# A graph network of two GINE and two GIN layers: edges counted in single tiles of 128, with up to 18 columns, and the units shared between the layers by columns

## The chip, the cores and the metric

The kernel runs on one core of a Trainium2 chip. The metric is the device time of one launch in microseconds (us), and lower is better. The core has five engines with an instruction queue each: TensorE (PE in the profile, with its weight loads as PEld), VectorE (DVE), ScalarE (ACT), GpSimd (POOL) and SyncE (SP). They wait for each other through semaphores. SP, ScalarE and GpSimd also issue transfers (DMA).

## The reference

There are N = 6250 nodes with D = 128 features, and E = 100,000 edges, sorted by their destination `dst`. Destinations are drawn as N times the square of a uniform number, so the first tiles of edges fall on few nodes and the last on more. With a layer norm and a ReLU before each half, it computes

```
h = max(layernorm(x), 0)
twice (GINE):  msg = relu(h[src] + edge_attr)              # one row of 128 per edge
               agg = segment_sum(msg, dst)
               h   = relu(relu(relu(batchnorm((h + agg) W1 + b1)) W2 + b2))
x = x + h
h = max(layernorm(x), 0)
twice (GIN):   agg = segment_sum(h[src], dst)               # no edge features
               h   = relu((1 + eps) h + agg) @ wA.T ... @ wB.T
x = x + h
```

A GINE message needs the row of its edge, so every edge's source row is gathered. A GIN message is just the source row: the sum over the edges is a product of node features with a matrix that says how many edges run from each node to each node. That matrix of counts depends on the edge list alone.

## The kernel before

*GINE layers.* Edges are taken in 98 groups of 1024 (128 partitions by G = 8 tiles). For every group, in this order: `load_rows` (SP) brings the edge features; `gather` (L638, GpSimd) issues eight indirect transfers of 128 rows into a `g` tile, of which there are eight; `places` (L647, VectorE) makes a one-hot matrix that says to which column (destination) each edge goes; `Counter.count` runs for the units that fall to this group; then `sums` adds the edge rows (L654, VectorE), applies the ReLU (L655, ScalarE) and multiplies with the one-hot on TensorE (L659, eight products in fp32, 16 passes). The sums are added into `acc`, which holds all nodes as columns, one group later (BEHIND = 1) at L690. Each engine keeps the order in which the program issues its instructions. A new gather into a `g` tile waits for the sums that read it eight groups earlier.

*Counting.* It runs beside the two GINE layers, for the first 70 groups' edges (560 tiles of 128), and prepares the GIN layers. A unit is a stretch of UE edges whose destinations span at most `plan.unit(u)` columns (at most WOVER). For each of its UT tiles, VectorE makes `lo_j` (L739: which of 128 places within a block of nodes the source has) and `at_j` (L742: which block of nodes and which column, 49 blocks by the unit's width). TensorE multiplies them (L754) into banks of 512 columns, of which there are three, so a unit takes one to three banks. The product is a matrix of counts, and VectorE adds it into the `win` tile at L730, at a column that it reads from a register. This addition is put off: `flush` for a unit is issued after the next unit's `lo_j` and `at_j` have been issued.

```
            self.at.ready(max(u - 1, 0))
            self.flush()
            ...
            for b in range(0, NB, per):
                n = min(per, NB - b)
                pa = bank_a()
                for j in range(UT):
                    nc.tensor.matmul(pa[:, : n * w], los[j], ats[j][:, b * w : (b + n) * w],
                                     start=j == 0, stop=j == UT - 1)
                self.late.append((u, b, n, w, pa))
```

A `win` tile covers a window of 256 destinations; there are 14 windows, two tiles, and ScalarE zeroes a tile (L716) before its next window, while SP stores the finished one. These clears and stores are chores, of which every unit issues two. Columns and registers come from `Places.ready` (L673): VectorE's queue loads eight values of a row (`urow` for units, `brow` for groups, `hrow` for windows) into registers, each with a check of its bounds.

*How the units are shared out.* Layer 0 counts the units before `half`, layer 1 the rest. Within a layer, `while u < last_u and (u - first_u) * (NG - 6) < (s + 1) * (last_u - first_u)` spreads them evenly over the first 92 groups.

*GIN layers.* TensorE multiplies the stored counts with the node features (L1047). The groups from the 70th on are still gathered.

*Preparation.* Before the first group, layer norm, index tables and the rows of registers are made (L427 to L566); `in_rows` (L455) turns columns into a row on one partition by products with the identity.

Of the kernel before, what the change touches and what calls it, by code (L numbers as in the profile page):

```python
# [9 lines left out]
F32 = mybir.dt.float32  # L10
# [4 lines left out]
ALU = mybir.AluOpType  # L15
AX = mybir.AxisListType

P = 128
# [13 lines left out]

KG = 70

UE = 256
UT = UE // P
UG = P * G // UE

WC = 256
WOVER = 30  # L40

QB = 7

# [1 line left out]
class Plan:  # L45
# [4 lines left out]
    def __init__(self, n_nodes: int, n_edges: int):  # L50
# [3 lines left out]
        while u < UG * KG:  # L54
            n = 1
            while u + n < UG * KG and self.reach(u * UE, (u + n + 1) * UE) <= WC:
                n += 1
# [18 lines left out]
    def unit(self, u: int) -> int:  # L76
        return min(WOVER, int(2 * np.ceil(self.reach(u * UE, (u + 1) * UE) / 2)))

# [5 lines left out]
def runs(widths):  # L84

    first = 0
    for i in range(1, len(widths) + 1):
        if i == len(widths) or widths[i] != widths[first]:
            yield first, i - first, widths[first]
            first = i  # L90
# [3 lines left out]
def gnn_kernel(ctx: ExitStack, tc: tile.TileContext, t: dict, out: bass.AP):  # L94
# [21 lines left out]
    nc = tc.nc  # L116
    x, src, dst, edge_attr = t["x"], t["src"], t["dst"], t["edge_attr_128"]
    N, E = x.shape[0], src.shape[0]
# [8 lines left out]
    NG = NGF + 1  # L127
# [8 lines left out]
    NU, NUA = KG * UG, NG * UG  # L136
# [3 lines left out]
    plan = Plan(N, E)  # L140
    windows = plan.windows
# [26 lines left out]
    code = big.tile([P, NT], F32)  # L168
    brow = const.tile([1, NG], I32)

    hrow = const.tile([1, len(windows)], I32)
# [11 lines left out]
    def chunks():  # L183

        for c in range(NCH):
            b0 = c * CB
            n0 = b0 * P
            yield c, b0, n0, min(CB * P, N - n0)
# [63 lines left out]
    def reached(end, places, edges):  # L252
        return next((at for at in places if plan.below(at * edges) >= end), None)

    gine_ends = {e: reached(e, range(1, NG), GE) for e in chunk_ends}
    counted_ends = {e: reached(e, [windows[c][0] for c in range(2, len(windows), 2)] + [NU], UE)
                    for e in chunk_ends}
    gathered_from = min(n0 for _, _, n0, _ in chunks() if n0 >= plan.above(NU * UE))

# [31 lines left out]
    def bank_e():  # L291
        return ps_e.tile([P, 512], F32, name="pe")
# [72 lines left out]
    class Steps:  # L365
# [19 lines left out]
        def end(self):  # L385
            while self.under_way:
                self.step()
# [4 lines left out]
    row = const.tile([P, 1], F32)  # L392
    nc.gpsimd.iota(row, pattern=[[0, 1]], base=-MID, channel_multiplier=1,
                   allow_small_or_imprecise_dtypes=True)
    for b in range(0, CODES, P):
        n = min(P, CODES + CODES % 2 - b)
# [30 lines left out]
    with tc.tile_pool(name="prep2", bufs=1) as pre2:  # L427
# [8 lines left out]
        lo, hi = ends[:, 3 : 3 + UG], ends[:, 3 + UG :]  # L436
# [14 lines left out]
        def in_rows(cols, name):  # L451

            p_r = bank_e()
            for i, col in enumerate(cols):
                nc.tensor.matmul(p_r[:1, i * NG : (i + 1) * NG], col, ident[:NG, :NG],  # L455
                                 start=True, stop=True)
            r = pre2.tile([1, len(cols), NG], F32, name=name)
            nc.vector.tensor_copy(r.rearrange("o c g -> o (c g)"), p_r[:1, : len(cols) * NG])
            return r

        of_group = in_rows([ends[:, i : i + 1] for i in range(3)] + [extra], "of_group")
        lo_r = in_rows([lo[:, i : i + 1] for i in range(UG)], "lo_r")
        hi_r = in_rows([hi[:, i : i + 1] for i in range(UG)], "hi_r")
        lo_u = pre2.tile([1, NUA], F32)
        nc.vector.tensor_copy(lo_u.rearrange("o (g h) -> o g h", h=UG), lo_r.rearrange("o h g -> o g h"))
        hi_u = pre2.tile([1, NUA], F32)
        nc.vector.tensor_copy(hi_u.rearrange("o (g h) -> o g h", h=UG), hi_r.rearrange("o h g -> o g h"))
        base_r, top_r = of_group[:, 0, :], of_group[:, 1, :]
        nc.vector.tensor_copy(brow, base_r)
        nc.vector.tensor_scalar_add(wrow, of_group[:, 3, :], 1.0)  # L470


# [19 lines left out]

        first_u = pre2.tile([1, NU], F32)
        for c, (a, n) in enumerate(windows):
            nc.vector.tensor_copy(hrow[:, c : c + 1], lo_u[:, a : a + 1])
            nc.vector.tensor_copy(first_u[:, a : a + n], lo_u[:, a : a + 1].to_broadcast([1, n]))
        nc.vector.scalar_tensor_tensor(diff_r[:, :NU], hi_u[:, :NU], -float(WC), first_u, op0=ALU.add,
                                       op1=ALU.subtract)
        worst(2, NU)

        n = NU - (2048 // UE - 2)
# [4 lines left out]
                                       op0=ALU.add, op1=ALU.subtract)  # L506
# [6 lines left out]
        for i, (u, end) in enumerate(early):  # L513
            nc.vector.tensor_scalar(diff_r[:, i : i + 1], lo_u[:, u : u + 1], -1.0, float(end - 1),
                                    op0=ALU.mult, op1=ALU.add)
# [4 lines left out]
        for s in range(NCH - 1 - BEHIND):  # L520
            u = UG * (s + 1) - 1
# [10 lines left out]
        def spread(r, n):  # L532

            p_b = bank_e()
            nc.tensor.matmul(p_b[:, :n], ones, r, start=True, stop=True)
            return p_b[:, :n]
# [6 lines left out]
        def by_tile(f, name):  # L543

            v = pre2.tile([P, KG, G], F32, name=name)
            for j in range(G):
                nc.vector.tensor_copy(v[:, :, j], transposed(f, j * P, 1, KG))
            return v

        s_t = by_tile(sg, "s_t").rearrange("p g j -> p (g j)")  # L550
        d_t = by_tile(dg, "d_t")
# [3 lines left out]
        block = pre2.tile([P, NT], F32)  # L555
        nc.vector.tensor_copy(block, block_i)
        nc.vector.scalar_tensor_tensor(slo, block, -float(P), s_t, op0=ALU.mult, op1=ALU.add)
        nc.vector.tensor_tensor(
            code.rearrange("p (u j) -> p u j", j=UT), d_t.rearrange("p g (h j) -> p (g h) j", j=UT),
            spread(lo_u[:, :NU], NU)[:, :, None].to_broadcast([P, NU, UT]), ALU.subtract)  # L560
        for a, n, w in runs([plan.unit(u) for u in range(NU)]):
            r = slice(a * UT, (a + n) * UT)
            nc.vector.scalar_tensor_tensor(code[:, r], block[:, r], float(w), code[:, r],
                                           op0=ALU.mult, op1=ALU.add)
# [9 lines left out]
    for name in vec_names:  # L574
        v = t[name]
        n = v.shape[0] if len(v.shape) == 2 else 1
# [24 lines left out]
    for name in ("eps1", "eps2"):  # L601
        e = t["L1_gnn_" + name]
# [60 lines left out]
    class Places:  # L663
# [5 lines left out]
        def ready(self, s):  # L669

            if s not in self.got:
                e = min(s + 8, self.row.shape[-1])
                _, got = nc.values_load_multi_w_load_instructions(  # L673
                    self.row[0:1, s:e], engines=[mybir.EngineType.DVE], min_val=0, max_val=self.most)
                self.got = dict(zip(range(s, e), got))

        def at(self, s, w):
# [19 lines left out]
    class Counter:  # L697
# [11 lines left out]
        def clear(self, c):  # L709

            if c < len(windows):
                win = self.wins[c] = self.pool.tile([P, NB, WC + WOVER], F16, name="win", bufs=2)
                flat = win.rearrange("p b w -> p (b w)").bitcast(F32)
# [231 lines left out]
    own_terms(tables[0], 1.0)  # L945
    rows, own_later = {}, []

    half = min((a for a, _ in windows), key=lambda a: abs(2 * a - NU))
    for l in range(2):

        first_stages, end = batch_norm(l)
        steps, rest = Steps(first_stages), list(chunks())
        cs = Columns(brow)
        u, first_u, last_u = (0, 0, half) if l == 0 else (half, half, NU)
        for s in range(NG):
            n = P if s < NGF else RP
            for r in range(l * NG + s, min(l * NG + s + AHEAD + 1, 2 * NG)):
                if r not in rows:
                    rows[r] = load_rows(gine, r % NG, P if r % NG < NGF else RP, AHEAD + 2)
            g = gather(edge, tables[l], n, srcs[:, s * G : (s + 1) * G], 8)  # L960
            onehot = places(edge, tables[l], dloc[:, s, :], plan.group(s))
            while u < last_u and (u - first_u) * (NG - 6) < (s + 1) * (last_u - first_u):
                counter.count(u)
                u += 1
                if u == NU:
                    counter.end()
            counter.some_chores()
            if own_later:

                got = None  # L970
                for stage in own_stages:
                    got = stage(*own_later[0], got)
                own_later.pop(0)
            cs.ready(max(s - BEHIND, 0))
            cs.later(s, sums(g, n, onehot, rows.pop(l * NG + s)), BEHIND)
            rows[l * NG + s] = None
            steps.step()
            ready = gine_ends[rest[0][2] + rest[0][3]]
            if ready is not None and ready <= s + 1 - BEHIND:
                steps.begin(rest.pop(0))  # L980
            if l == 0 and s == AHEAD:
                unplanned = nc.values_load(total[0:1, 0:1], min_val=0, max_val=1)
        if l:
            ahead[:] = chunks()
            load_ahead(x)
        while cs.late:
            cs.add(*cs.late.pop(0))
        for chunk in rest:
            steps.begin(chunk)
            steps.step()  # L990
        steps.end()
        if l == 0:
            own_stages = gine_nodes(0, *end())[:3]
            staged(*gine_rows(tables[1], own_stages[0]))
            own_later = list(chunks())
# [13 lines left out]
    queue, tiles = [(l, c, q) for l in range(2) for c, q in order], {}  # L1009
# [82 lines left out]
    for l in range(2):  # L1092
# [37 lines left out]
        for s in range(KG, NG):  # L1130
            n = P if s < NGF else RP
            g = gather(gin, tables[2 + l], n, srcs[:, s * G : (s + 1) * G], 4)
# [107 lines left out]
```

## Time and profile before

| what | us |
|---|---|
| median of 3 runs | 3341.68 (3339.88 to 3350.18) |
| the profiled execution's own time | 3338.77 |
| its span, first to last instruction | 3336.8 |
| first gather of GINE layer 0, last gather | 41.4, 1195.8 |
| first gather of GINE layer 1, last gather | 1267.3, 2434.7 |
| last addition into `acc` of layer 1 | 2471.6 |
| TensorE, VectorE, ScalarE, GpSimd busy | 1820.7, 1382.5, 455.4, 2035.1 |

The mean TensorE clock that was granted is 0.764 of full speed. The first 148 us or so are preparation, 41 to 2472 us the two GINE layers with the counting beside them (their start overlaps with the preparation), and the rest the GIN layers.

How to read the profile: a row of the costliest groups has the line, the engine, the operation, output <- inputs, the shape and the number of instructions; after the bar, busy time in all, mean ns of one, and idle time of the engine just before them with what ended most of it. "Issue" means that nothing the profile shows was waited for, and "remote" that the waking event belongs to no engine the profile can name. In the waits a row says which instruction waited for which, how long in total, how often, and the longest. In the timeline a line has the start, the duration (several instructions in one line are joined), the engine and line, and in brackets the idle time before and its releaser. Ends of matmuls are modelled.

### The profile page before, as it was taken

What the parts mean: (1) busy time and instruction counts of PE and PEld (TensorE: products, weight loads), DVE (VectorE), ACT (ScalarE), POOL (GpSimd) and SP (SyncE); (2) the same over time, 40 slices, a digit from 0 to 9 for tenths busy, and PEclk for the clock granted to TensorE, in tenths of its full rate; (3) what the DMA queues carried; (4) which work ended last, traced back from release to release, by engine and by line L of the source; (5) the groups of instructions that cost most, each with busy time, mean ns of one, the idle gap of its engine ahead of it and who ended that gap; (6) DMA issues with size and microseconds to landing.
All of it is one profiled execution on the core that took longest, in us unless ns stands there. A gap on an engine that the chain in (4) does not pass through costs nothing. (4 is left out here: it accounts for less than half of the span.)

```text
span 3336.8 us, 28904 instructions
## 1 busy us (share of the span) xinstructions
PE 1820.7 (55%) x8459; PEld 1143.3 (34%) x8460; DVE 1382.5 (41%) x3051; ACT 455.4 (14%) x579; POOL 2035.1 (61%) x2118
## 2 busy tenths in 40 slices
PE   1333424444444453365555564455558688857997
PEld 0233423332323242243333343332334344423443
DVE  5322424334445542255555666677753111211112
ACT  1200101010101121111101111111122101110000
POOL 6467666666667736666766666666614566545662
PEclk9999999995666665555555656666778888878998
DMA  3332323234224224242442443343447455545664
GB/s 117 121 95 89 100 79 95 88 92 127 90 88 134 90 69 139 69 128 89 135 128 82 128 134 119 118 133 119 125 136 236 137 170 185 184 136 183 224 219 128
DMA packets 259236, 421.94 MB, mean 126 GB/s; under 512 B 40864, under 2 KB 187088, under 8 KB 259068
## 3 DMA queue, kind: packets, MB, share of 16 engines
q1 hardware_dynamic: 173532, 184.05, 17.8%
q0 software_dynamic: 71424, 146.03, 14.7%
q10 hardware_dynamic: 14112, 89.92, 7.6%
q8 instruction: 69, 1.13, 0.1%
q14 instruction: 99, 0.81, 0.1%
HBM read 352.48 MB, written 67.36 MB: 126 GB/s over the span
## 5 line engine op out<-in xcount | busy, mean ns | idle before, releaser
L638 POOL DMA_INDIRECT g<-table,srcs x2016 | 1982.6, 983 | 1095.2 <-issue 913.2
L659 PE MATMUL pe<-onehot,g 128*128 128x16 f32 (+25 forms) x4480 | 751.8, 338 | 603.8 <-ACT g L655 339.7
L659 PEld LDWEIGHTS pe<-onehot,g 128*128 128x128 f32 x3136 | 621.7, 300 | 657.7 <-ACT g L655 406.3
L754 PE MATMUL pa<-at_j,lo_j 128*128 128x450 f16 (+22 forms) x1172 | 423.1, 488 | 644.1 <-DVE win L730 246.8
L1047 PE MATMUL pa<-piece,xp 128*128 128x512 f16 x2058 | 496.8, 394 | 75.7 <-issue 73.3
L730 DVE TENSOR_TENSOR win<-win,pa 128x450 f32 (+17 forms) x586 | 316.3, 574 | 494.9 <-remote 363.7
L754 PEld LDWEIGHTS <-lo_j 128*128 128x128 f16 x1172 | 155.0, 138 | 858.0 <-issue 521.8
L655 ACT ACTIVATE g<-g 128x1024 f32<-128x1024 f32 x196 | 207.0, 1056 | 1599.2 <-DVE g L654 773.9
L742 DVE TENSOR_SCALAR at_j<-numbers,code 128x1470 f16<-128x1470 f16 (+13 forms) x560 | 362.9, 648 | 0.0
L690 DVE TENSOR_TENSOR acc<-acc,pe 128x112 f32 (+18 forms) x252 | 61.2, 243 | 692.4 <-remote 288.6
L1047 PEld LDWEIGHTS <-xp 128*128 128x128 bf16 x2058 | 204.0, 100 | 360.7 <-issue 155.2
L654 DVE TENSOR_TENSOR g<-g,rows 128x1024 f32<-128x1024 f32 x196 | 238.8, 1218 | 81.1 <-issue 46.1
L647 DVE TENSOR_TENSOR onehot<-numbers,dloc 128x896 bf16<-128x896 f32 (+23 forms) x252 | 224.4, 890 | 9.0 <-issue 9.0
L739 DVE TENSOR_SCALAR lo_j<-numbers,slo 128x128 f16<-128x128 f16 x560 | 153.5, 274 | 2.1 <-issue 2.1
L659 PEld LDWEIGHTS <-g 128*128 128x128 bf16 (+1 forms) x1344 | 87.9, 103 | 80.5 <-issue 57.3
L716 ACT COPY win<-zero 128x1001 f32<-128x1001 f32 x98 | 92.9, 1018 | 74.0 <-remote 74.0
L690 DVE TENSOR_TENSOR acc<-acc,pa 128x256 f32 x28 | 11.8, 422 | 180.2 <-PE pa L1047 109.0
L799 DVE BATCH_NORM_STATS2 bst<-pn 128x6 f32<-128x512 f32 (+1 forms) x26 | 17.3, 666 | 164.7 <-remote 89.4
L918 ACT ACTIVATE y<-pn,vcols 128x512 f32<-128x512 f32 (+1 forms) x26 | 17.1, 658 | 473.3 <-PE pn L331 421.7
L319 POOL TENSOR_SCALAR h<-xs,rs 128x128 f32<-128x128 f32 x49 | 21.3, 447 | 90.7 <-DVE rs L312 84.5
L826 DVE TENSOR_TENSOR xs<-xs,pn 128x512 f32<-128x512 f32 (+1 forms) x26 | 17.0, 654 | 71.0 <-PE pn L347 44.0
L1101 DVE TENSOR_TENSOR h<-pn,xp 128x512 f32<-128x512 f32 (+1 forms) x13 | 8.6, 658 | 90.8 <-ACT xp L1100 68.5
(162 smaller groups left out, 640.8 us busy)
## 6 DMA issues: line engine op xcount, KB each, us to landing
rows<-in_edge_attr SPq DMA_DIRECT2D x194, 512.0 KB
piece<-counts ACTq DMA_DIRECT2D x98, 896.0 KB
counts<-win SPq DMA_DIRECT2D x98, 448.0 KB
g<-table,srcs POOLq DMA_INDIRECT x2016
table<-xp SPq DMA_DIRECT2D x24, 384.0 KB
x_first<-in_x SPq DMA_DIRECT2D x8, 384.0 KB
table<-x_first SPq DMA_DIRECT2D x8, 384.0 KB
xs<-table SPq DMA_DIRECT2D x12, 256.0 KB
```

The lines of the kernel that those rows point to most:

```text
L638: nc.gpsimd.indirect_dma_start(out=g[:n, j, :], out_offset=None, in_=table, in_offset=bass.IndirectOffsetOnAxis(ap=idx[:n, j : j + 1], axi ...
L647: nc.vector.tensor_tensor(onehot, cols[:, None, :w].to_broadcast([P, G, w]), dl[:, :, None].to_broadcast([P, G, w]), ALU.is_equal)
L654: nc.vector.tensor_add(g[:n], g[:n], rows[:n])
L655: nc.scalar.activation(g[:n], g[:n], AF.Relu)
L659: nc.tensor.matmul(pe, g[:n, j, f : f + D], onehot[:n, j, :], start=(j, f) == terms[0], stop=(j, f) == terms[-1])
L690: nc.vector.tensor_add(a, a, sums)
L716: self.chores.append(lambda v=flat[:, q * n : (q + 1) * n], n=n: nc.scalar.copy(v, self.zero.to_broadcast([P, n])))
L730: nc.vector.tensor_add(v, v, pa[:, : n * w].rearrange("p (b w) -> p b w", w=w))
L739: nc.vector.tensor_scalar(lo_j, cols16[:, MID : MID + P], slo[:, col : col + 1], None, op0=ALU.is_equal)
L742: nc.vector.tensor_scalar(at_j[:, :width], cols16[:, :width], code[:, col : col + 1], None, op0=ALU.is_equal)
L754: nc.tensor.matmul(pa[:, : n * w], los[j], ats[j][:, b * w : (b + n) * w], start=j == 0, stop=j == UT - 1)
L1047: nc.tensor.matmul(pa, xp[:, q * QB + b, i * D : (i + 1) * D], v[:, :, b, :], start=q + b + i == 0, stop=q == NQ - 1 and b == QB - 1 and i ...
```

## The change

A unit becomes one tile of 128 edges (UE = 128, UT = 1), so there are 560 units where there were 280, and its width is at most 18 columns where it was at most 30. Widths are now 4, 6, ... 18 along the edges, where they were 4 to 30. A unit takes one bank up to width 10 and two above. `at_j` and `lo_j` have two buffers each where they had four (2 * UT). The `win` tile is 274 columns wide for each block where it was 286.

Units are shared out by cost, where a unit's cost is its width plus 3. Layer 0 now takes 343 of the 560 tiles and layer 1 217; before, it was 132 units (264 tiles) and 148 units (296 tiles). Within a layer the units are spread over the groups by the same cost.

The rows of registers are clamped to their bounds on the chip where they are made (`brow`, `hrow`; `urow` was already), and the loads of registers skip their check.

In the preparation, the rows of first and last destinations of the units are made in two pieces each, since a bank holds five rows of 98, and the code of each tile is made in pieces of 512 units.

```diff
-UE = 256
+UE = 128
 UT = UE // P
 UG = P * G // UE
 
 WC = 256
-WOVER = 30
+WOVER = 18
...
-        lo_r = in_rows([lo[:, i : i + 1] for i in range(UG)], "lo_r")
-        hi_r = in_rows([hi[:, i : i + 1] for i in range(UG)], "hi_r")
-        lo_u = pre2.tile([1, NUA], F32)
-        nc.vector.tensor_copy(lo_u.rearrange("o (g h) -> o g h", h=UG), lo_r.rearrange("o h g -> o g h"))
-        hi_u = pre2.tile([1, NUA], F32)
-        nc.vector.tensor_copy(hi_u.rearrange("o (g h) -> o g h", h=UG), hi_r.rearrange("o h g -> o g h"))
+
+        def of_units(v, name):
+
+            row = pre2.tile([1, NUA], F32, name=name)
+            h = 512 // NG
+            for i in range(0, UG, h):
+                k = min(h, UG - i)
+                part = in_rows([v[:, j : j + 1] for j in range(i, i + k)], f"{name}_{i}")
+                nc.vector.tensor_copy(row.rearrange("o (g h) -> o g h", h=UG)[:, :, i : i + k],
+                                      part.rearrange("o h g -> o g h"))
+            return row
+
+        lo_u, hi_u = of_units(lo, "lo_u"), of_units(hi, "hi_u")
         base_r, top_r = of_group[:, 0, :], of_group[:, 1, :]
-        nc.vector.tensor_copy(brow, base_r)
+        nc.vector.tensor_scalar(brow, base_r, float(N), 0.0, op0=ALU.min, op1=ALU.max)
...
-            nc.vector.tensor_copy(hrow[:, c : c + 1], lo_u[:, a : a + 1])
+            nc.vector.tensor_scalar(hrow[:, c : c + 1], lo_u[:, a : a + 1], float(N), 0.0,
+                                    op0=ALU.min, op1=ALU.max)
...
-        nc.vector.tensor_tensor(
-            code.rearrange("p (u j) -> p u j", j=UT), d_t.rearrange("p g (h j) -> p (g h) j", j=UT),
-            spread(lo_u[:, :NU], NU)[:, :, None].to_broadcast([P, NU, UT]), ALU.subtract)
+        for a in range(0, NU, 512):
+            n = min(512, NU - a)
+            tiles = slice(a * UT, (a + n) * UT)
+            nc.vector.tensor_tensor(
+                code[:, tiles].rearrange("p (u j) -> p u j", j=UT),
+                d_t.rearrange("p g j -> p (g j)")[:, tiles].rearrange("p (u j) -> p u j", j=UT),
+                spread(lo_u[:, a : a + n], n)[:, :, None].to_broadcast([P, n, UT]), ALU.subtract)
...
                 _, got = nc.values_load_multi_w_load_instructions(
-                    self.row[0:1, s:e], engines=[mybir.EngineType.DVE], min_val=0, max_val=self.most)
+                    self.row[0:1, s:e], engines=[mybir.EngineType.DVE], min_val=0, max_val=self.most,
+                    skip_runtime_bounds_check_because="the row is clamped to these bounds on chip")
...
-    half = min((a for a, _ in windows), key=lambda a: abs(2 * a - NU))
+    cost = np.cumsum([0] + [plan.unit(u) + 3 for u in range(NU)])
+    half = min((a for a, _ in windows), key=lambda a: abs(2 * cost[a] - cost[NU]))
     for l in range(2):
...
-            while u < last_u and (u - first_u) * (NG - 6) < (s + 1) * (last_u - first_u):
+            while u < last_u and (cost[u] - cost[first_u]) * (NG - 6) < (s + 1) * (
+                    cost[last_u] - cost[first_u]):
                 counter.count(u)
                 u += 1
```

## The prediction

> **What bounds the kernel now.** I read the page's costliest groups, then the busy time by stretch, then the waits, and last the timeline.
>
> ```profile
> L638 POOL DMA_INDIRECT g<-table,srcs x2016 | 1982.6, 983 | 1095.2 <-issue 913.2
> L754 PE MATMUL pa<-at_j,lo_j 128*128 128x450 f16 (+22 forms) x1172 | 423.1, 488 | 644.1 <-DVE win L730 246.8
> L730 DVE TENSOR_TENSOR win<-win,pa 128x450 f32 (+17 forms) x586 | 316.3, 574 | 494.9 <-remote 363.7
> L690 DVE TENSOR_TENSOR acc<-acc,pe 128x112 f32 (+18 forms) x252 | 61.2, 243 | 692.4 <-remote 288.6
> ```
>
> GpSimd issues eight gathers per group of 1024 edges. A gather takes 0.94 us and the next starts 0.30 us later, so a group costs at least 10.0 us there. Beside it run the row addition, the sums and the counting. The busy time by stretch, for two stretches of each GINE layer (PE, PEld, DVE, ACT, POOL):
>
> ```profile
> 225.00:791.00 566.00, 231.70 (x942) 186.76 (x943) 201.23 (x507) 52.73 (x52) 387.98 (x392) 0.97 0.32 97
> 791.00:1118.00 327.00, 139.41 (x618) 101.30 (x618) 157.25 (x329) 45.44 (x47) 228.02 (x225) 0.63 0.32 100
> 1426.00:1588.00 162.00, 92.17 (x336) 59.01 (x336) 88.70 (x188) 28.79 (x33) 110.52 (x112) 0.54 0.36 110
> 1588.00:2347.00 759.00, 416.03 (x1606) 266.75 (x1606) 482.86 (x888) 121.88 (x126) 503.33 (x505) 0.60 0.39 121
> ```
>
> Divide each length by its groups (gathers over eight): 11.55, 11.63, 11.57 and 12.02 us a group, while VectorE is busy 4.1, 5.6, 6.3 and 7.65 us of it. No engine is full, and more VectorE work hardly shows until the last stretch. What fills the rest is in the waits:
>
> ```profile
> DVE win L730 <- remote: 363.7, 48, 23.1
> DVE acc L690 <- remote: 330.0, 24, 43.1
> ```
>
> "Remote" names no engine. The timeline shows what it is:
>
> ```profile
> 368.27 3.48 PE L659 MATMUL pe<-onehot,g 128*128 128x40 f32 x16
> ...
> 388.11 0.20 DVE L690 TENSOR_TENSOR acc<-acc,pe 128x40 f32 x1 [21.99 <-remote]
> ...
> 388.82 0.94 POOL L638 DMA_INDIRECT g<-table,srcs  x1 [4.40 <-issue]
> ```
>
> TensorE had done these sums by 371.8, but VectorE goes on only at 388.11, after GpSimd ran out of free g buffers and stood 4.40 us. The recorded increments of TensorE's semaphore come 3.5 to 6.3 us apart from 370 to 387, then 0.04 us apart. So the work falls into clear stretches, in which hand-overs are prompt, and blocked ones, in which TensorE's completions are posted late until GpSimd stalls. GpSimd stalls over 1 us 33 times in layer 0 (4.39 us on average over its normal step) and 46 times in layer 1 (3.39). The other delays of gathers come to 32 to 34 us a layer, so a group costs about 10.3 us of gathering plus its share of a stall: over a layer's 98 groups 10.3 + 33x4.39/98 = 11.8 and 10.3 + 46x3.39/98 = 11.9. The number of stalls sets the pace.
>
> In a clear stretch a group with two units looks like this:
>
> ```profile
> 389.98 1.20 DVE L654 TENSOR_TENSOR g<-g,rows 128x1024 f32<-128x1024 f32 x1
> ...
> 391.26 1.06 ACT L655 ACTIVATE g<-g 128x1024 f32<-128x1024 f32 x1 [24.00 <-DMA g<-table,srcs]
> ...
> 392.37 3.63 PE L659 MATMUL pe<-onehot,g 128*128 128x40 f32 x16 [2.27 <-ACT g L655]
> ...
> 395.81 1.18 PE L754 MATMUL pa<-at_j,lo_j 128*128 128x294 f16 x4
> 396.54 0.46 DVE L730 TENSOR_TENSOR win<-win,pa 128x294 f32 x1 [2.60 <-PE pa L754]
> 397.01 1.23 DVE L654 TENSOR_TENSOR g<-g,rows 128x1024 f32<-128x1024 f32 x1
> ```
>
> The next row addition is queued on VectorE behind the window addition of the group's first unit, whose matmul is queued on TensorE behind the last group's sums: 7.03 us from addition to addition, in series. A group with one unit flushes a unit whose matmul precedes those sums; its row addition does not wait, and two groups are in flight. The shortest intervals between row additions, stretch by stretch of 14 groups, are in layer 0 2.4 to 4.5 us with one unit and 7.0 to 8.0 with two (middle 3.5 and 7.5), in layer 1 4.1 to 6.0 and 8.3 to 10.2 (5.1 and 9.2). All intervals: in layer 0 17.8 mean with two units (39 groups), 6.9 with one (52); in layer 1 16.7 (56) and 7.6 (36).
>
> **What the Trainium skill says.** "TensorE: Matmul & The Clock Gate", The cost: per-tile semaphore tail: increments on completion serialize at 26.3 ns each. The trace agrees in clear stretches (0.04 us) and is a hundred times off in blocked ones. "GPSIMD Engine Reference", Specifications: GpSimd shares its SBUF interfaces with VectorE. The trace fits: a gather beside a row addition takes 1.94 us (390.06). "VectorE: DVE Perf Modes", Why PSUM operands drop a tier: a PSUM operand halves the fast rate, and fp32 runs at one. The rows agree: at_j (fp16) has a slope of 0.52 ns per column, the window addition 0.87.
>
> **The change part by part.** Counted from the plan, which fixes widths and order.
>
> *Less column work.* at_j has 295,960 columns where it had 474,712. By the rows (0.207 + 0.00052 us per column for at_j, 0.234 + 0.00087 for an addition) counting costs VectorE 291 -> 440 us in layer 0 and 569 -> 436 in layer 1: level in sum, moved to layer 0. VectorE's whole work per group becomes about 7.4, 7.0, 6.7, 7.2 us along layer 0 and 6.9 in layer 1 (late layer 1 had 7.65 to 9.6). On VectorE's load alone, late layer 1 falls from 12.02 to 11.6: 0.42 us x 63 groups = -27 us. I take -10, since this stretch also has longer chains than the others; kept: -30 to 0. Matmuls go from 372 to 397 and from 800 to 434.
>
> *More hand-overs.* 280 units become 560. Units per group: layer 0 from 1.43 to 5.6, 4.5, 3.4, 2.8 (14, 14, 35, 29 groups); layer 1 from 1.6 to 2.36. So every group now has two or more, and every row addition stands behind a window addition that waits for the last group's sums. A further narrow unit adds lo_j 0.19, at_j 0.28, addition 0.38 (start to start near 392) = 0.85 us; with two banks about 1.4 to 1.5. Clear chain in layer 0: 7.0 + 3.6x0.85 = 10.1; 7.0 + 2.5x0.85 = 9.1; 7.4 + 1.4x1.4 = 9.4; 7.6 + 0.8x1.5 = 8.8; weighted 9.3, where it was 0.57x3.5 + 0.43x7.5 = 5.2. Layer 1: about 8.4 (two banks to add in place of three) + 0.36x1.9 = 9.1, where it was 0.4x5.1 + 0.6x9.2 = 7.6.
>
> *What that does to stalls.* Two estimates. (1) Groups per stall are 98/33 = 2.97 at a chain of 5.2 and 98/46 = 2.13 at 7.6. If a clear stretch lasts U and p groups get through a blocked one: U/5.2 + p = 2.97, U/7.6 + p = 2.13, so U = 13.8, p = 0.31. At 9.3: 1.79 groups, 55 stalls, +22x4.39 = +97 us in layer 0. At 9.1: 1.83, 54 stalls, +8x3.39 = +27 in layer 1. (2) By waits: 48 remote waits at window additions in 95 two-unit groups are 0.5 per such group; 184 such groups give 92, and the 24 at acc vanish, being covered. 92/2 = 46 per layer: +13x4.39 = +57 and 0. I take between: +77 and +13 = +90.
>
> *Asserts.* The 560 of them go:
>
> ```profile
> L673 DVEq FUSED_REGOPS  x560: 2/183/1396, 141.0 to 3294.8; - x187
> L673 DVEq SEQ_ASSERT  x560: 1/23/710, 141.3 to 3295.0; - x187
> ```
>
> At 0.28 us a pair that is up to 151 us of VectorE's queue, but the chain shows 1% for it, and the queue waits anyway. 35 more urow loads at 0.6 us come in. I take -8; kept: -25 to +10.
>
> *Preparation.* Longer rows (560 for 280 elements), some twelve operations by 0.29 us = +3.5 us on VectorE, hidden: it waits 37.6 us for TensorE at 102.5. Five fewer code transposes, eight more one-row products on TensorE. Taken 0; uncovered +3.
>
> *Clears and stores.* 98 copies shrink from 1001 to 959 elements and the chores come two per unit, thus bunched; ScalarE is 14% busy. Taken 0. The GIN stage keeps its order.
>
> Sum: 3338.8 - 10 + 90 - 8 + 3 = 3414 on the profiled execution. It is 3 us below the median of 3341.7, so about 3415 to 3417; I say 3415, with 3350 to 3490 for this case.
>
> **The rivals.**
> (A) Faster: VectorE's load is what lifts late layer 1, and stalls don't follow the chain. For it: 12.02 at the heaviest load. Against: flat elsewhere. 3338.8 - 27 - 8 = 3304; 3285 to 3330. It decides if fewer than three stalls are added.
> (B) No change: gathering hides all. For it: 11.55, 11.63, 11.57 at chains from about 5 to 7. Against: no stretch yet had a chain of 9. 3333 to 3350.
> (C) Much slower: every group behaves as two-unit groups after two-unit groups did (18 in layer 1, 13.7 us). (13.7-11.6)x92 + (13.7-12.0)x92 = +350: 3690. Against: those are picked out of a sequence in which one-unit groups follow at 7.3.
>
> **How the numbers follow.** Main case 0.58, A 0.24, B 0.11, C 0.07. A measurement here can tell 0.3%, about 10 us. Range: 3303 leaves out the lower half of A; the upper end 3520 takes in the main case with estimate (1) in full and early layer 0 at its 10.1 us chain, and leaves out C. Faster 0.25, same 0.11, slower 0.64.
>
> **What would show it.** Right: more than 45 GpSimd stalls in layer 0, pace above 12.2 us a group there, window additions holding nearly all remote waits and the acc additions few, layer 1 within 0.3 us of 12. Wrong: layer 0 at 11.6 (A or B), stalls below 35, or intervals in early layer 0 near 17 (C). If VectorE's idle time on "remote" falls in layer 0, the steps on stalls have failed.

## The result: no change, and the profile after

| | us |
|---|---|
| before, median of 20 runs | 3351.17 (3339.56 to 3366.42) |
| after, median of 20 runs | 3350.96 (3338.47 to 3358.48) |
| after / before | 0.9999, 95% interval 0.9985 to 1.0013 |
| span of the profiled execution, after | 3356.3 |

The forecast was 3415 with 3303 to 3520, slower at 0.64. The time lies in the range, but the change did not move it.

A spread of 20 to 27 us lies within each kernel's runs, and the one profiled execution of before is among its quickest, that of after among its slower ones. So 20 us between the two spans mean nothing, and only differences by stage are read here, where a second trace of after shows them too.

The costliest groups of the page of after, those that answer to the rows of before:

```profile
L650 POOL DMA_INDIRECT g<-table,srcs x2016 | 1972.5, 978 | 1124.2 <-issue 935.6
L743 DVE TENSOR_TENSOR win<-win,pa 128x196 f32 (+11 forms) x831 | 421.0, 532 | 933.0 <-remote 660.9
L703 DVE TENSOR_TENSOR acc<-acc,pe 128x112 f32 (+18 forms) x252 | 61.0, 242 | 329.1 <-PE pn L331 85.3
```

The idle time of VectorE has moved from the additions into acc (692 us before, 329 after) to the window additions (495 before, 933 after). The waits of after say the same:

```profile
DVE win L743 <- remote: 660.9, 81, 43.9
...
DVE acc L703 <- remote: 129.6, 9, 42.6
```

Together 90 waits of 8.8 us, where there were 72 of 9.6. The busy time by stretch (PE, PEld, DVE, ACT, POOL), for the same four stretches of time:

```profile
225.00:791.00 566.00, 255.56 (x972) 184.93 (x972) 275.73 (x742) 58.97 (x59) 383.83 (x382) 1.00 0.34 101
791.00:1118.00 327.00, 152.72 (x566) 109.49 (x566) 165.25 (x354) 44.28 (x47) 223.71 (x224) 0.58 0.37 110
1426.00:1588.00 162.00, 85.41 (x311) 57.83 (x312) 75.14 (x183) 37.48 (x45) 103.48 (x107) 0.51 0.36 106
1588.00:2347.00 759.00, 361.16 (x1347) 252.69 (x1347) 394.26 (x803) 110.68 (x115) 505.40 (x515) 0.53 0.39 115
```

That is 11.85, 11.68, 12.11 and 11.79 us a group, where it was 11.55, 11.63, 11.57 and 12.02. Layer 0 and early layer 1 lost, late layer 1 gained. From first to last gather, layer 0 took 1187.6 us (1154.4 before) and layer 1 1149.9 (1167.4).

A stall is counted here as in the prediction: the step from one gather's start to the next is over 1 us longer than the normal 1.24 us. GpSimd stalled 43 times in layer 0 (33 before; 171.0 us over the normal step against 144.9) and 42 in layer 1 (46; 146.3 against 155.7). A second trace of after gave 42 and 44. This count takes in a few gathers that were themselves stretched to nearly 2 us, with no pause behind them. Pauses of over 1 us, from one gather's end to the next one's start, are 41 in layer 0 (26 before; 168.8 us against 137.3) and 42 in layer 1 (41; 145.8 against 148.8). So the pauses grew by 31 us in layer 0 and hardly changed in layer 1. Of the 17.5 us that layer 1 gained, 13 are fewer stretched gathers: those over 1.05 us exceed the normal 0.94 us by 26 us in all, where it was 39. What stretches them is shown further down.

The timeline of after shows one blocked group and one clear one of four units:

```profile
341.29 1.22 DVE L666 TENSOR_TENSOR g<-g,rows 128x1024 f32<-128x1024 f32 x1
...
355.93 0.46 DVE L743 TENSOR_TENSOR win<-win,pa 128x294 f32 x1 [11.68 <-remote]
356.60 0.94 POOL L650 DMA_INDIRECT g<-table,srcs  x1 [3.29 <-issue]
...
358.60 1.23 DVE L666 TENSOR_TENSOR g<-g,rows 128x1024 f32<-128x1024 f32 x1 [0.40 <-issue]
...
364.92 0.55 DVE L743 TENSOR_TENSOR win<-win,pa 128x294 f32 x1 [3.32 <-PE pe L671]
...
367.10 1.21 DVE L666 TENSOR_TENSOR g<-g,rows 128x1024 f32<-128x1024 f32 x1
```

The clear group takes 8.5 us and waits at the window addition behind the sums, as the prediction's chain has it. The group before it lost 11.68 us at the same place, and VectorE went on only when GpSimd had stood for most of the 3.29 us. What the prediction had wrong is what this adds up to.

### The profile page after: what moved, and what is told of

It reads as the page before. It is cut to its first block, busy times and chain, and to the rows that moved or that the text cites. A ratio compares the mean times of both kernels' runs of the same rounds, so it can differ in the third digit from the quotient of the medians.

```text
span 3356.3 us, 27793 instructions
## 1 busy us (share of the span) xinstructions
PE 1794.5 (53%) x8131; PEld 1138.5 (34%) x8132; DVE 1372.9 (41%) x3279; ACT 451.4 (13%) x579; POOL 2025.0 (60%) x2118
## 4 chain that ended last, share of the span: by engine, by line
PE 26%; issue 20%; another core or an unknown queue 20%; POOL 13%; DVE 11%; ACT 4%; DMA 4%; DVEq 1%; ACTq 0%; SPq 0%; POOLq 0%
POOL g L650 12%; PE pa L1062 11%; PE pe L671 10%; DMA g<-table,srcs 3%; DVE win L743 2%; ACT g L667 2%; DVE at_j L755 2%; DVE g L666 2%; DVE onehot L659 2%; PE pa L767 1%; PE pn L331 1%; DVE lo_j L752 1%; ACT win L729 1%; DVEq L743 1%
## 5 line engine op out<-in xcount | busy, mean ns | idle before, releaser
L671 PE MATMUL pe<-onehot,g 128*128 128x16 f32 (+25 forms) x4480 | 807.3, 356 | 550.3 <-issue 266.3
L671 PEld LDWEIGHTS pe<-onehot,g 128*128 128x128 f32 x3136 | 664.6, 320 | 839.9 <-ACT g L667 417.7
L743 DVE TENSOR_TENSOR win<-win,pa 128x196 f32 (+11 forms) x831 | 421.0, 532 | 933.0 <-remote 660.9
L767 PE MATMUL pa<-at_j,lo_j 128*128 128x196 f16 (+11 forms) x831 | 336.0, 471 | 744.0 <-DVE at_j L755 277.9
L767 PEld LDWEIGHTS <-lo_j 128*128 128x128 f16 x831 | 110.4, 147 | 691.0 <-DVE at_j L755 422.6
L755 DVE TENSOR_SCALAR at_j<-numbers,code 128x490 f16<-128x490 f16 (+7 forms) x560 | 270.8, 484 | 0.0
L729 ACT COPY win<-zero 128x959 f32<-128x959 f32 x98 | 89.2, 984 | 75.5 <-DVE zero L956 75.5
```

The lines of the kernel that those rows point to most:

```text
L671: nc.tensor.matmul(pe, g[:n, j, f : f + D], onehot[:n, j, :], start=(j, f) == terms[0], stop=(j, f) == terms[-1])
L729: self.chores.append(lambda v=flat[:, q * n : (q + 1) * n], n=n: nc.scalar.copy(v, self.zero.to_broadcast([P, n])))
L743: nc.vector.tensor_add(v, v, pa[:, : n * w].rearrange("p (b w) -> p b w", w=w))
L755: nc.vector.tensor_scalar(at_j[:, :width], cols16[:, :width], code[:, col : col + 1], None, op0=ALU.is_equal)
```

## The experiments

Two kinds of chip. The experiments fell on seven chips. On two of them the kernel before took about 3350 us, as in the measurement above, and the traces show late completions of TensorE and GpSimd's stalls. On the other five it took 2802 to 2810 us. None of the 13 traces from there has a wait on "remote", and GpSimd stalls at most eleven times in both layers together; most of these are stretched gathers, and pauses of over 1 us are at most four. The completions themselves differ too. In the GINE layers of the kernel before (late), 643 of 1898 recorded increments of TensorE's semaphore come over 1 us after the nearest earlier end of a matmul that makes one; in the single tiles alone (prompt) none of 2490 does. The ends are modelled, but the starts are recorded: in the prediction's example the last of the sums has started by 371.4 us, and their increments come until 388.5. I call them late and prompt chips. No chip was measured at two times, so whether this lasts on a chip is not known.

Each ratio is against the kernel before on the same chip; ratios of the two kinds are not mixed. Letters in the expectations (A and C are not the rivals A and C of the prediction): S, GpSimd's stalls set the pace whatever the counting's size; L, VectorE's load does; A, the checks left out give back what the units cost; C, the order (row additions behind window additions) sets the stalls; H, the number of hand-overs does; T, the single tiles cost what the other parts gain.

### Parts of the change alone, late chip

*Loads without checks*, in the kernel before (with the clamps of the change):

```diff
-                    self.row[0:1, s:e], engines=[mybir.EngineType.DVE], min_val=0, max_val=self.most)
+                    self.row[0:1, s:e], engines=[mybir.EngineType.DVE], min_val=0, max_val=self.most,
+                    skip_runtime_bounds_check_because="the row is clamped to these bounds on chip")
```

> The kernel before, its rows of registers clamped and its register loads without checks: that part of the change alone. Theory A: faster, 0.985 to 0.995 of before. Theory S: the queue's work is hidden, 0.998 to 1.002.

Measured 0.9932 (0.9908 to 0.9957), -23 us. The register loads in its trace, by operation:

```profile
L674 DVEq TENSOR_LOAD <-urow x35: 593/597/1912, 141.7 to 2363.3; - x35
L674 DVEq TENSOR_LOAD <-brow x34: 537/598/3850, 150.5 to 3278.0; - x34
L674 DVEq TENSOR_LOAD <-hrow x4: 602/740/834, 2530.5 to 3193.0; - x4
```

Not only the 560 asserts have gone but also the 560 register operations beside them. "Hidden" (S) was wrong: 23 of at most 151 us showed.

*Shares by columns*, units of 256:

```diff
-    half = min((a for a, _ in windows), key=lambda a: abs(2 * a - NU))
+    cost = np.cumsum([0] + [plan.unit(u) + 3 for u in range(NU)])
+    half = min((a for a, _ in windows), key=lambda a: abs(2 * cost[a] - cost[NU]))
...
-            while u < last_u and (u - first_u) * (NG - 6) < (s + 1) * (last_u - first_u):
+            while u < last_u and (cost[u] - cost[first_u]) * (NG - 6) < (s + 1) * (
+                    cost[last_u] - cost[first_u]):
```

> The kernel before, units of 256, with the units shared by columns as in the change: that part alone. Theory L (VectorE's load in late layer 1 costs time): 0.988 to 0.996. Theory A: 0.997 to 1.003, since VectorE has idle time in both layers.

Measured 0.9918 (0.9891 to 0.9946), -28 us. In its trace layer 1 took 1140.6 us with 37 stalls, layer 0 1178.6 with 47. So moving columns to layer 0 costs time there and saves it in layer 1, which fits L. But in this pair of traces, the slowest of its four runs and a quick one of before, the two cancel: 2319 us for both layers against 2322. Where the 28 us lie is not shown.

*The whole change again:*

> The kernel after itself, beside the kernel before on one chip. Where TensorE's completions come promptly (before near 2808 us) theory A (single-tile units cost what the checks left out give back) has 0.997 to 1.002, since with the checks back it was 1.014; if it is above 1.01 the checks are worth little and the single tiles cost. Where they come late (before near 3350 us) 0.997 to 1.003 again, 40 to 46 stalls of GpSimd in layer 0.

Measured 1.0014 (1.0001 to 1.0027), 42 stalls in layer 0, as expected. Two parts gain 0.7 and 0.8%, the whole nothing. If the parts add up, the single tiles cost 1.0014 / (0.9932 x 0.9918) = 1.017 there. That they add up is not shown, and on prompt chips they do not (below).

### The order of row addition and counting

In these the row addition and the ReLU are issued ahead of the group's counting:

```diff
             onehot = places(edge, tables[l], dloc[:, s, :], plan.group(s))
+            with_rows(g, n, rows.pop(l * NG + s))
...
-            cs.later(s, sums(g, n, onehot, rows.pop(l * NG + s)), BEHIND)
+            cs.later(s, sums(g, n, onehot, None), BEHIND)
```

(`with_rows` holds the two operations that `sums` had.) In the kernel before, late chip:

> The kernel before with row addition and ReLU issued ahead of the group's counting. Theory C (row additions standing behind window additions cost time in two-unit groups): 0.985 to 0.996 where completions are prompt, less than 0.98 where they come late. Otherwise 0.998 to 1.002.

Measured 0.9932 (0.9910 to 0.9955), between the expectations for a late chip, with 37 and 43 stalls (33 and 46 before): not through fewer stalls. Where its gain comes from stays open; the gap between the layers' gathers is 56.3 us (61 to 72 in the late-chip traces of the old order).

In the single tiles alone (shares by count, loads checked), which fell on a late chip:

> The kernel after with checked register loads, shares by count, and row additions ahead of the counting: single tiles alone, in the other order. Where completions are prompt: if the cost of 1.0% comes through row additions that land late and stretch gathers, it goes: 0.995 to 0.999 of before, under 40 us of stretching. If it comes from the counting's own size or the checks: 1.005 to 1.01. Where completions come late (before near 3350 us): 0.985 to 0.997 if the order is the cause, 1.003 to 1.015 if the number of hand-overs is.

Measured 1.0014 (1.0000 to 1.0028), between the two expectations. Against 0.9932 for units of 256 in the same order, on the other late chip, single tiles cost 0.8%. Its waits:

```profile
DVE win L746 <- remote: 574.8, 77, 33.0
DVE acc L706 <- remote: 210.7, 10, 60.7
```

No row addition stands behind a window addition of its own group here, and 87 remote waits remain, with 35 and 48 stalls. The shortest interval between row additions of a three-unit group in layer 0 is 3.4 us (7.9 in the change, whose three-unit groups are wider), and yet the mean is 11.3 (11.5). The order is not what makes the stalls: C fails on late chips.

### Prompt chips

The single tiles alone (shares by count, loads checked; the clamps of the rows and the pieces of the preparation stay as in the change):

```diff
-UE = 256
+UE = 128
...
-WOVER = 30
+WOVER = 18
```

> The kernel after with checked register loads and shares by count: single tiles with up to 18 columns alone. Theory T: 1.012 to 1.022 of before. If the single tiles cost nothing by themselves and a gain of the other parts was lost in their combination: 0.997 to 1.004.

> The kernel after with checked register loads and shares by count: single tiles alone. Where completions come late (before near 3350 us), theory T (the parts add up, 1.0014 over 0.993 x 0.992): 1.012 to 1.02, with 45 or more stalls of GpSimd in layer 0. If the parts don't add up: 0.998 to 1.008. Where they are prompt: 1.009 again.

> The kernel after with checked register loads and shares by count: single tiles alone. Where completions come late (before near 3350 us), theory T (the parts add up): 1.012 to 1.02 of before; if they don't add up 0.998 to 1.008. Where they are prompt, 1.010 once more.

Measured 1.0092 (1.0075 to 1.0109), 1.0103 (1.0087 to 1.0119) and 1.0099 (1.0082 to 1.0115); and in a fourth run 1.0103 (1.0084 to 1.0122):

> The kernel after with checked register loads and shares by count: single tiles alone. Where completions come late (before near 3350 us): if the three parts of the change add up to its 1.0014, 1.012 to 1.02; if the single tiles cost there what they cost with the row additions ahead, 1.006 to 1.01; if nothing, 0.998 to 1.003. Where they are prompt: 1.010 again, and the question stays open.

All fell on prompt chips, so the single tiles alone in the order of the change were never measured on a late one. On prompt chips they cost 1.0%, between the two ranges of the first expectation. The change without its single tiles:

> The kernel before with units of 256, but shared by columns and with register loads without checks: the change without its single tiles. Theory T (the single tiles cost about what the two other parts gain, and the parts add up): 0.993 x 0.992 = 0.985 of before, 0.981 to 0.989. If the two parts gain from the same waits (theory S) and don't add up: 0.990 to 0.994.

Measured 0.9994 (0.9984 to 1.0004), outside both ranges: the two parts, which gain 0.7 and 0.8% alone on a late chip, gain nothing together on a prompt one. The whole change:

> The kernel after. Where completions are prompt (before near 2805 us): 1.0037 (old shares) x 1.0137/1.0092 (shares by columns against by count, both with checks) = 1.008, 1.004 to 1.011. If the gathers' pace hid everything: 0.999 to 1.003. Where they come late (before near 3350 us): 0.998 to 1.003 once more.

Measured 1.0048 (1.0033 to 1.0064): here it is a loss, as expected. The parts do not add up: 1.010 for the single tiles times 0.9994 for the rest would be 1.009. With the old shares:

> The kernel after, with the units shared between and within the layers by count, as before. Theory S (GpSimd's stalls set the pace, about one per 2.3 groups, whatever the counting's size): 0.997 to 1.005 of before, 38 to 46 stalls in each layer. Theory L (VectorE's load sets it: moving columns to layer 0 cost there what it gained in layer 1): layer 0 near 11.55 us a group again, late layer 1 near 12.0, and slower than the kernel after by 10 to 20 us only if layer 1's gain was real.

Measured 1.0037 (1.0023 to 1.0051), so the shares do next to nothing there. The ratio lies in S's range, but the 38 to 46 stalls did not come: three and one, all of them stretched gathers. With the checks back:

> The kernel after, with the bounds checks of the register loads back. Theory A (the single-tile units cost some 30 us and the checks left out gave them back): 1.008 to 1.02 of before. Theory S: 0.997 to 1.005, the queue's work hidden in VectorE's waits.

Measured 1.0137 (1.0118 to 1.0156), against 1.0048 without: on prompt chips the checks cost 0.9% with single tiles, where 840 of them run (560 with units of 256). Shared by count, with the checks in, it was 1.010 (the single tiles alone above), so with checks the shares by columns cost 0.4%. Without any counting (no lo_j, at_j, matmuls, window additions or registers, windows stored as zeros):

> The kernel after, with the counting itself left out (no lo_j, at_j, matmuls, window additions or their registers; the windows are cleared and stored as zeros, so the GIN sums are incomplete). Theory L: no load, so the pace falls to gathering, 10.0 to 10.3 us a group, 3050 to 3120 us. Theory S: GpSimd still stalls, over 20 times in each layer, pace 10.8 to 11.5 us, 3180 to 3300 us.

Measured 0.9929 (0.9911 to 0.9947), 2789 us, without a pause of over 1 us. The expectations were times of a late chip, but as ratios (0.91 to 0.93, 0.95 to 0.985) both fail too. Each layer takes 991 us there, 10.1 us a group, which is the 10.0 of gathering alone: without late completions gathering is the bound, and a kernel without any counting is only 0.7% faster than before (1.2% faster than the change). And the change with row additions first:

> The kernel after, with a group's row addition and ReLU issued ahead of its counting, so that no row addition stands behind a window addition. Theory C (the clear chain from row addition to row addition decides how often GpSimd stalls, the prediction's step): 25 to 35 stalls in each layer, 0.97 to 0.985 of before. Theory S: the stalls follow late completions of TensorE and not this order, 38 to 46 stalls, 0.997 to 1.005.

> The kernel after with row additions ahead of the counting. Theory C (the single tiles' loss comes from row additions standing behind the group's window additions): the whole loss comes back, 0.980 to 0.987 of before. Theory H (it comes from the number of hand-overs between VectorE and TensorE itself): the same gain as in the kernel before and no more, 0.992 to 0.998.

> The kernel after with row additions ahead of the counting. Where completions come late, theory C (the single tiles' cost comes through the order): 0.98 to 0.988 of before; theory H (it comes from the number of hand-overs): 0.992 to 0.998. Where they are prompt, 0.996 once more.

Measured 0.9955 (0.9941 to 0.9969), 0.9962 (0.9947 to 0.9976) and 0.9962 (0.9948 to 0.9975): faster than both kernels on prompt chips (the change itself is at 1.0048), so here the order gets back more than the whole loss. C's and S's ranges missed, and the second and third run fell where H and the forecast for prompt chips had them. Where the time goes is in the gathers' row of the page. Of the change:

```profile
L650 POOL DMA_INDIRECT g<-table,srcs x2016 | 1963.5, 974 | 674.7 <-issue 618.7
```

Of the change with row additions first:

```profile
L650 POOL DMA_INDIRECT g<-table,srcs x2016 | 1938.7, 962 | 673.2 <-issue 597.7
```

And without counting:

```profile
L650 POOL DMA_INDIRECT g<-table,srcs x2016 | 1931.0, 958 | 671.0 <-issue 600.8
```

25 us of gathering lie between the first two, which differ in the order alone, and the two ratios, 1.0048 and 0.9962 on two prompt chips, differ by 24 us. The single tiles alone, whose gathers are stretched most, show in the timeline how it happens:

```profile
740.89 0.63 DVE L742 TENSOR_TENSOR win<-win,pa 128x392 f32 x1 [1.76 <-issue]
741.41 1.20 DVE L666 TENSOR_TENSOR g<-g,rows 128x1024 f32<-128x1024 f32 x1
741.58 1.85 POOL L650 DMA_INDIRECT g<-table,srcs  x1 [0.30 <-issue]
```

And that of the change with row additions first:

```profile
742.77 0.94 POOL L650 DMA_INDIRECT g<-table,srcs  x1 [0.30 <-issue]
742.95 1.23 DVE L665 TENSOR_TENSOR g<-g,rows 128x1024 f32<-128x1024 f32 x1 [4.26 <-DMA g<-table,srcs]
744.02 0.97 POOL L650 DMA_INDIRECT g<-table,srcs  x1 [0.30 <-issue]
```

A gather that is due while a row addition runs takes longer by about the rest of that addition: 1.85 us for 0.94. A row addition released by its last gather's landing starts just after a gather has started and is done as the next one starts: 0.97. Of the single tiles' 118 gathers of over 1.05 us in the two layers, 116 started during a row addition; of the 143 during which a row addition began, none took longer than 0.96. These 118 lie 71 us over the normal in all; in the change it is 119 and 54; in the change with row additions first 65 and 29; with shares and no checks on units of 256 63 and 31. The waits of the change say why:

```profile
DVE win L743 <- PE pa L767: 401.0, 163, 7.1
DVE g L666 <- DMA g<-table,srcs: 285.8, 108, 13.4
```

Against those of the change with row additions first:

```profile
DVE g L665 <- DMA g<-table,srcs: 655.0, 161, 15.6
...
DVE win L747 <- PE pa L771: 14.3, 17, 1.4
```

In the change, 84 of the 196 row additions follow a window addition at once, at any moment of a gather, and 35 of the 54 us of stretching are theirs; in the other order none does, and 161 come when their data lands. The prediction's chain is shown here, by another price: stretched gathers, not stalls. The Trainium skill, "GPSIMD Engine Reference", Specifications, says that GpSimd shares its SBUF interfaces with VectorE. The trace fits, and adds that it is the gather starting during a row addition that pays.

All three gains together, units of 256:

> The kernel before with all three: shares by columns, loads without checks, row additions issued ahead of the counting. If the gains add up: 0.978 (0.972 to 0.984); if the order of the row additions gains from the same waits: 0.983 to 0.988.

Measured 0.9989 (0.9981 to 0.9998), outside both ranges: on a prompt chip there is next to nothing to regain with units of 256. So the order is worth 0.9% with single tiles (1.0048 to 0.9962) and nothing with units of 256 (0.9994 to 0.9989), and H's same gain in both fails as well. In the new order the single tiles are even the faster ones, by 0.3% (0.9962 against 0.9989, on one chip). Units of 256 with all three were not run on a late chip.

## Why the prediction was wrong, by its own steps

*What bounds the kernel.* The reading (gathering plus stalls) holds for the trace it was made from, with a blemish: 13 of its 79 stalls were stretched gathers. That the stalls come on some chips alone no single trace could show; elsewhere the same kernel runs at 2805 us, and the traces from there have next to none. The increments of a burst lie 0.04 us apart, which the prediction calls agreement with 26.3 ns; it is half as much again.

*More hand-overs, the clear chain.* Right in kind, and somewhat too long in size: predicted 10.1 us for 5.6 units and 9.1 for 4.5; shortest in the trace 9.3 for five or six and 8.4 for four. For layer 1 9.1 was predicted; shortest are 6.7 with two units and 8.7 with three.

*What that does to stalls* is the step that failed: +77 us in layer 0 and +13 in layer 1 were taken, and between the two traces layer 0 took 33 us more and layer 1 17.5 less. Estimate (2) was close in its counts: 92 remote waits at window additions and none at acc (81 and 9 measured), 46 stalls per layer (43 and 42). So the signs named beforehand came in part: the waits as told, the stalls and the pace of layer 0 just short (43 for over 45, 12.1 us a group for over 12.2). Estimate (1), that a longer chain lets fewer groups through a clear stretch, was wrong: 55 and 54. Groups per stall in layer 0 are 98/43 = 2.3 in the change, and with the shortest chains of all (single tiles with row additions first) 98/35 = 2.8, no more than the 3.0 before. I took the middle of the two. And the price was wrong: 4.39 us a stall was held fixed, but stalls shortened to 3.98, so ten more in layer 0 added 26 us, where +77 was taken. In layer 1 they fell by four, -9 us, where +13 was taken. By pauses alone it is 15 more, each shortened from 5.3 to 4.1 us (+31), and one more (-3). Why a pause gets shorter when there are more of them was not tested.

*Less column work* and *asserts* were undersized: -10 and -8 taken, -28 and -23 measured for shares and checks alone, with units of 256, on a late chip. The argument that the register queue waits anyway was the error in the second. What single tiles cost there follows only if the parts add up: +1.7%, some 55 us; with row additions first, 0.8% was measured. The sum of my terms was +75; the whole measured is nothing. The stretched gathers, 78 us over both layers before and 67 after, were counted among stalls and other delays and held fixed.

*The rivals of the prediction.* B had the number (no change) with a wrong cause: gathering does not hide all, since two parts alone gain 0.7 and 0.8%. That the single tiles' cost and these gains balance is the likely reading, not a shown one. A's mechanism, load, would be one of the gains. C's 13.7 us a group did not come.

What stays open: the single tiles alone on a late chip in the order of the change, whether the parts add up there, a kernel without counting there, and what makes TensorE's completions late on some chips.

## What to carry to other kernels

Test the parts of a change one by one: here two parts gained 0.7 to 0.8% each on a late chip, and together with the third nothing was left. An operation that slows the bounding engine's next instruction should be released by the event that sets its phase (here the landing of the gathered rows), not by work queued ahead of it: that was worth 0.9% of the change's time on prompt chips. Before stalls are counted, pauses and stretched instructions should be told apart. And before a stall is priced, see whether it is there on another chip.

## What the runs showed of the hardware that was not expected

- The same kernel took 3350 us on two chips and 2805 us on five. In the late traces, TensorE's semaphore increments came up to 6.3 us apart while GpSimd issued gathers (kernel before, 370 to 387 us), then 0.04 us apart once GpSimd paused. The part after the last gather of layer 1 differs too: 902 to 915 us against 716 to 727.
- A gather due during a row addition (fp32, both inputs in SBUF, 1.2 us) is stretched by about the rest of it, from 0.94 to up to 2.03 us; one that has already started when the row addition begins is not, but for three in 20 traces. Gathers over 1.05 us come to 18 to 88 us over the normal in all, by order, unit size and chip.
- Leaving out the checks of register loads took 560 asserts and 560 register operations from VectorE's queue (units of 256, late chip), worth 0.7% of the time; putting 840 of each back cost 0.9% (single tiles, prompt chip).
